# A row LSTM on one core: the gate product of the even pixels on GpSimd, the residual on VectorE, and a new written order

## The chip, the core and the metric

The kernel runs on one core of a Trainium2 chip. A core has five engines with a queue of instructions each: TensorE (PE in the profile; its weight loads stand apart as PEld), VectorE (DVE), ScalarE (ACT), GpSimd (POOL) and SyncE (SP), which here only issues the DMA transfers. The engines wait for each other through semaphores. Tiles lie in SBUF, or in PSUM, into which TensorE writes. The metric is the device time of one execution in microseconds, as the median of several runs. The profile shows another single execution, with its own time.

## What is computed

The input `x` is 8 images of 96 channels and 128 x 128 pixels in fp32. It is normalised in groups of three channels, goes through an LSTM that walks down the rows, and the LSTM's output is added to `x`:

```python
def step(carry, row_in):                       # one image row at a time
    h, c = carry
    ss = conv1d(h, W_ss, padding=1) + b_ss     # 3 taps along the row, 96 -> 384 channels
    gates = ss + row_in                        # row_in: masked 1x3 convolution of the normalised row
    f, i, o = sigmoid(...), sigmoid(...), sigmoid(...)
    g = tanh(...)
    c_new = f * c + i * g
    h_new = o * tanh(c_new)
    return ((h_new, c_new), h_new)
x = x + lstm(group_norm(x))
```

Row r needs `h` of row r-1, so the 128 rows are strictly in sequence. The mask leaves of `row_in` the left and the middle tap.

## The kernel before

**Half-steps.** The 8 images are two streams `s` of four. A half-step `n` is one row of one stream: `row, s = divmod(n, 2)`, 256 of them. While one stream's row is on TensorE, the other's is in the gates. Four rows are a block `k`, loaded from and stored to memory together.

**Tiles of the gates.** The 384 gate channels are permuted into three PSUM banks of 128 rows: A has the forget gate in rows 0 to 95, B the input gate, C the output gate, and rows 96 to 127 of each hold a third of `g`. A bank has 512 columns: even pixels of four images, then odd pixels.

**Fewer products.** The three-tap convolution for a pair of an even and an odd pixel is written with sums and differences of `h`: `vs` (even + odd), `vf` (their difference) and `vd` (two shifted differences). Product `1` (weights times `vs`) and product `2` (`vf`) go into the first and second half of a bank. Then ScalarE copies the first half to SBUF with the bias (`cp`, L508), VectorE writes the sum of both back as the even half (`lo`, L512) and the difference as the odd half (`hi`, L516), and products `0` and `3` (`vd`) are added to these halves by TensorE. The normalised row enters in the same form (`P`, `Q` before the copy, `E` after it), from operands `xs`. Channels 64 to 95 of the row share the contraction with `h` in rows 96 to 127 of `hx` ("shared" rows); channels 0 to 63 stand in `xs` ("own" images).

**Two halves of the array.** Each product is split into two of 64 contraction rows. `Lanes` deals them alternately to the upper and the lower half of TensorE's array, which work side by side. A half-step has 33 such products, each two records in the profile. Where both halves add into one bank, a wait keeps them in sequence.

**The written order.** Within the main loop nothing is planned by a scheduler: `PERIOD` (L678) lists every instruction of a half-step, and `do` (L698) issues them in that order to the engines' queues. A name is a part and a tile: `1A` is product 1 of tile A; `fg` is `forget`, f * c; `gt` is `gated`, i * g; `ce` is `cell`, c = f * c + i * g; `th` is its tanh; `ou` is `output`, o * tanh, which writes `h` into `hx`; `S` is `total` (`vs`), `F` is `difference` (`vf`), `D` is `shifted` (`vd`, on GpSimd); `re` is `residual`. A trailing `a` or `b` is the half of the even or odd pixels. A prime means the half-step before, `+` the next, `*` the one after that; `S`, `F` and `D` are made for the stream's next row.

**GpSimd's queue.** In each half-step it makes `vd` (L589), adds the residual (L607), and at `W` prepares the next block (`prepare`): of one image it normalises four rows into `xw` (`widen`, L297), forms sum (L315) and differences (L316) into `xs` (`combine`), and it normalises shared rows of one image into `hx` (`normalise_shared`); in the half-steps of a block's first row, also one row of image 3. `finish` stores a block after its fourth row's residual and loads the block after the next. `shifted` waits until VectorE is done with `S` and `F`. `FIRST` spreads the preparation of the first blocks by hand over half-steps 0 to 7.

Of the kernel before, what the change touches and what calls it, by code (L numbers as in the profile page):

```python
# [8 lines left out]
AF = mybir.ActivationFunctionType  # L9
# [12 lines left out]
def kernel(  # L22
# [32 lines left out]
    nc = tc.nc  # L55
    B, C, H, W = x.shape
    P = 128
    NH = 2
    BH = B // NH
# [239 lines left out]
    def widen(engine, xw, i, n, s, k, j, lo, step=1):  # L299


        norm(
            engine,
            strided(xw[:, i, :], 0, [(step * (W + 1), n), (J + 1, 2), (1, J)]),
            (x0[:, 0, j] if s == 1 and k == lo == 0 else xr[s][:, j, lo * W : (lo + n) * W])
            .rearrange("p (r j t) -> p r t j", r=n, t=2),
            0,
            1,
            s * BH + j,
        )  # L310

    def combine(xw, n, total, differences):

        e, o = xw[:, 0:n, 0:J], xw[:, 0:n, J + 1 :]
        nc.gpsimd.tensor_add(total, e, o)  # L315
        nc.gpsimd.tensor_sub(  # L316
            differences,
            strided(xw[:, 0, :], 0, [(W + 1, n), (J, 2), (1, J)]),
            strided(xw[:, 0, :], J + 1, [(W + 1, n), (0, 2), (1, J)]),
        )  # L320

    def own_image(s, k, j):

# [11 lines left out]
            to[:, r, 1:3, lo:hi].rearrange("p t b j -> p b t j"),  # L335
        )

    normalised = {}

    def normalise_shared(engine, s, k, j, lo, hi):  # L340

        normalised[s, k] = norm(
            engine,
            strided(
                hx[s][k % 2][C:P, lo, 0, j, :],
                0,
                [(2 * BH * JP, hi - lo), (BH * JP + 1, 2), (1, J)],
            ),
            (x0[C:P, 1, j : j + 1] if s == 1 and k == lo == 0 else xt[s, k][C:P, j, lo:hi, :])
            .rearrange("p r (j t) -> p r t j", t=2),  # L350
            C,
            0,
            s * BH + j,
        )
# [17 lines left out]
    class Lanes:  # L372
# [21 lines left out]
        def wait(self, number):  # L394

            if number > self.waited:
# [5 lines left out]
                )  # L402
                self.waited = number

    lanes = Lanes()
    whole = slice(0, P)

    class HalfStep:


        def __init__(self, n):
            self.n, (self.row, self.s) = n, divmod(n, NH)
            self.ps, self.m1, self.moving, self.done, self.gates, self.th = {}, {}, {}, set(), None, None
            self.started, self.images, self.halves, self.writer = set(), {}, {}, {}
            self.hx = hx[self.s][self.row // R % 2][:, self.row % R]
            self.xs = xs[self.s][self.row // R % 2][:, self.row % R]
            self.c = cs[self.s].rearrange("p t b j -> p (t b j)")
# [102 lines left out]
            nc.scalar.activation(self.part(g, lo, hi, t), self.part(ps, lo, hi, t), AF.Tanh)  # L520


        def sigmoid(self, a):
            if self.row == 0 and a == 0:
                return
            gate = self.ps[a][0:C]
            nc.scalar.activation(gate, gate, AF.Sigmoid)  # L527

        def forget(self):
            f = self.ps[0][0:C]  # L530
# [3 lines left out]
        def gated(self, lo=0, hi=BH, t=None):  # L534
            to = self.g if self.row > 0 else self.c
            to, i, g = (self.part(ap, lo, hi, t) for ap in (to, self.ps[1][0:C], self.g))
            nc.vector.tensor_mul(to, i, g)  # L537


        def part(self, ap, lo, hi, t=None):  # L540
# [30 lines left out]
        def total(self, engine=nc.vector, lo=0, hi=BH):  # L571
            e, o = self.pair(lo, hi)
            self.last = engine.tensor_add(self.operand("vs")[:, 0, lo:hi], e, o)  # L573
            row, s = divmod(self.n + 1, NH)
            if engine is nc.vector and row >= R and row % R < 2 and (s, row // R) in normalised:
                tc.add_manual_dep(
                    self.last.ins,
                    normalised[s, row // R].ins.name,
                    mybir.DependencyInfo(mybir.DependencyClass.Sync, mybir.DependencyReason.DATA),
                    reason="the next difference finds the next rows of x normalised",  # L580
                )

        def difference(self, engine=nc.vector, lo=0, hi=BH):
            e, o = self.pair(lo, hi)
# [2 lines left out]
        def shifted(self, lo=0, hi=BH):  # L587
            h = self.hx[:, 0, lo, :]
            diff = nc.gpsimd.tensor_sub(  # L589
                self.operand("vd", 2)[:, :, lo:hi],  # L590
                strided(h, 1, [(BH * JP - 1, 2), (JP, hi - lo), (1, J)]),
                strided(h, 0, [(BH * JP + 1, 2), (JP, hi - lo), (1, J)]),
            )
            if self.last.ins.engine != E.Pool:
                tc.add_manual_dep(
                    diff.ins,
                    self.last.ins.name,
                    mybir.DependencyInfo(
                        mybir.DependencyClass.Sync, mybir.DependencyReason.SCHED_ONLY
                    ),  # L600
                    reason="GpSimd starts when VectorE is done with both SBUF reads",
                )

        def residual(self):
            s, row = self.s, self.row
            xo = xt[s, row // R][0:C, :, row % R, :].rearrange("p b (j t) -> p t b j", t=2)
            (nc.gpsimd if 2 * row + s < last else nc.vector).tensor_add(xo, xo, self.h)  # L607

    def store(s, k, lo, hi):
        nc.sync.dma_start(  # L610
# [6 lines left out]

    SHARED = (((0, 0, R), (3, 0, 1)), ((1, 0, R),), ((2, 0, R),), ((3, 1, R),))

    def own(s, *images):  # L620
        return [(own_image, s, 1, j) for j in images]

    def shared(s, k, *images):
        return [
            (normalise_shared, nc.gpsimd, s, k, *(j if isinstance(j, tuple) else (j, 0, R)))
            for j in images
        ]

    FIRST = [
        own(0, 0),  # L630
        own(0, 1),
        own(0, 2) + shared(0, 1, 0, 1),
        own(0, 3) + [(load_rows, 0, 2)] + shared(0, 1, 2, 3),
        own(1, 0, 1),
        own(1, 2) + shared(1, 1, 0, 1),
        own(1, 3) + [(load_rows, 1, 2)] + shared(1, 1, 2, 3),
        [(own_image, 0, 2, 0), (own_image, 1, 2, 0)],
    ]

    def work(n):  # L640
        if n < len(FIRST):
            return FIRST[n]
        row, s = divmod(n, NH)
        k, r = divmod(row, R)
        parts = []
        if r == R - 1 and k + 2 < NB:
            parts.append((own_image, s, k + 2, 0))
        elif r < R - 1 and k + 1 < NB:
            parts.append((own_image, s, k + 1, r + 1))
        if k + 1 < NB:  # L650
            parts += shared(s, k + 1, *SHARED[r])
        if r == R - 2 and k + 2 < NB:
            parts.append((load_rows, s, k + 2))
        return parts

    worked = set()

    def prepare(n):
        if n not in worked:
            worked.add(n)  # L660
            for part, *args in work(n):
                part(*args)

    def finish(n):
        prepare(n)
# [18 lines left out]
    SPLIT = ("taC", "gt", "ce", "th", "ou")  # L684
    PARTS = {
# [317 lines left out]
```

## Time and profile before

| | us |
|---|---|
| median of 3 runs | 2023.72 (2023.52 to 2024.3) |
| the profiled execution, its own time | 2027.04 |
| its span | 2025.2 |
| TensorE busy | 1923.3 |
| VectorE busy | 1529.1 |
| ScalarE busy | 1494.9 |
| GpSimd busy | 1473.1 |
| granted TensorE clock | 0.997 |

A group of the profile has the line of the code, the engine, the operation, the names of the written and read tiles with buffer numbers left out, their shape, and count, busy time and mean duration. A timeline gives the start in us from the span's start, the duration, and the instructions merged if neighbours are alike (`x2`); in brackets stands the idle time before, with the instruction that ended it. Records of one engine may overlap[...]. TensorE's busy time says little alone: its records overlap in pairs.

### The profile page before, as it was taken

To read this page: it belongs to the slowest core of one execution; us is meant where nothing else is said; L and a number is where in the kernel's file an instruction comes from. 1 tells how busy PE (TensorE), PEld (TensorE's weight loads), DVE (VectorE), ACT (ScalarE), POOL (GpSimd) and SP (SyncE) were. 2 spreads that over 40 slices of the span, in tenths; PEclk is the share of its full clock that TensorE was granted. 3 is DMA by queue.
4 is the path that set the end of the run, shared out by engine and by line. 5 is a ranking of instruction groups with operands and counts; after the bars stand their busy time and mean duration, and the time that the engine had idled before them with its cause. 6 is when DMAs were issued, how large, how long until landed. Compare 5 with 4: busy or idle time off the path is not lost.

```text
span 2025.2 us, 44842 instructions
## 1 busy us (share of the span) xinstructions
PE 1923.3 (95%) x16936; PEld 1831.0 (90%) x16936; DVE 1529.1 (76%) x3996; ACT 1494.9 (74%) x3161; POOL 1473.1 (73%) x1712
## 2 busy tenths in 40 slices
PE   0289999999999999999999999999999999999998
PEld 0178999999999999999999999999999999999997
DVE  5767777777777777777777777777777777777776
ACT  3776777777777777777777777777777777777776
POOL 3348777777777777777777777777777777777752
PEclk9989999999999999999999999999999999999999
DMA  9994333444334334433433443343344333434411
GB/s 374 424 310 100 98 103 91 112 115 104 82 89 113 92 101 115 113 83 82 110 95 95 116 116 95 79 100 96 93 116 116 96 82 96 107 92 106 116 33 32
DMA packets 103382, 237.11 MB, mean 117 GB/s; under 512 B 5952, under 2 KB 8896, under 8 KB 97280
## 3 DMA queue, kind: packets, MB, share of 16 engines
q1 hardware_dynamic: 103168, 234.25, 42.0%
q8 instruction: 135, 2.21, 0.5%
q14 instruction: 79, 0.65, 0.1%
HBM read 183.90 MB, written 50.33 MB: 116 GB/s over the span
## 4 chain that ended last, share of the span: by engine, by line
PE 93%; DMA 4%; ACT 2%; DVE 1%; issue 0%; SPq 0%; POOL 0%; DVEq 0%; POOLq 0%
PE ps L442 92%; DMA piece<-in_x_dram 3%; DMA xs<-in_x_dram 1%; ACT piece L216 1%; PE ps L174 0%; ACT piece L217 0%; DVE bst L876 0%; ACT hx L295 0%; ACT piece L295 0%; DVE hx L560 0%; ACT xs L216 0%; ACT xs L217 0%; SPq L864 0%; PE pv L251 0%; DVE ps L516 0%
## 5 line engine op out<-in xcount | busy, mean ns | idle before, releaser
L442 PE MATMUL ps<-vd,wl 64*128 64x256 f32 (+1 forms) x6096 | 1390.9, 379 | 0.3
L442 PEld LDWEIGHTS ps<-vd,wl 64*128 64x128 f32 (+1 forms) x6096 | 1028.4, 186 | 45.7 <-issue 2.4
L442 PE MATMUL ps<-vs,wm 64*128 64x256 f32 (+1 forms) x3052 | 775.1, 380 | 4.9 <-POOL vs L573 4.4
L442 PE MATMUL ps<-vf,wm 64*128 64x256 f32 (+1 forms) x3052 | 766.3, 377 | 0.0
L527 ACT ACTIVATE ps<-ps 96x512 f32<-96x512 f32 x766 | 441.6, 577 | 356.2 <-PE ps L442 348.1
L442 PE MATMUL ps<-xs,wx 64*128 64x256 f32 x3080 | 637.8, 377 | 11.1 <-POOL xs L315 11.1
L589 POOL TENSOR_TENSOR vd<-hx 128x512 f32<-128x512 f32 x257 | 266.7, 1038 | 388.5 <-PE ps L442 384.8
L442 PEld LDWEIGHTS ps<-xs,wx 64*128 64x128 f32 x3080 | 494.0, 187 | 14.2 <-POOL xs L315 11.6
L520 ACT ACTIVATE g<-ps 32x256 f32<-32x256 f32 (+1 forms) x1021 | 468.6, 482 | 26.7 <-PE ps L442 6.3
L442 PEld LDWEIGHTS ps<-vf,wm 64*128 64x128 f32 (+1 forms) x3052 | 475.4, 187 | 11.0 <-PE ps L442 0.4
L442 PEld LDWEIGHTS ps<-vs,wm 64*128 64x128 f32 (+1 forms) x3052 | 459.6, 186 | 21.6 <-POOL vs L573 5.4
L512 DVE TENSOR_TENSOR ps<-m,ps 128x256 f32<-128x256 f32 x768 | 326.0, 425 | 192.5 <-ACT m L508 182.0
L442 PE MATMUL ps<-xs,wt 64*128 64x256 f32 x1530 | 453.2, 377 | 0.6 <-DVE ps L516 0.6
L508 ACT ACTIVATE m<-ps,wl 128x256 f32<-128x256 f32 x766 | 361.6, 474 | 90.9 <-PE ps L442 84.3
L532 DVE TENSOR_TENSOR ps<-ps,c 96x512 f32<-96x512 f32 x254 | 176.8, 696 | 232.9 <-PE ps L442 226.9
L607 POOL TENSOR_TENSOR x<-x,hx 96x512 f32<-96x512 f32 x255 | 330.8, 1297 | 6.7 <-DVE hx L560 6.7
L516 DVE TENSOR_TENSOR ps<-m,ps 128x256 f32<-128x256 f32 x768 | 300.8, 422 | 1.3 <-PE ps L442 1.2
L442 PEld LDWEIGHTS ps<-xs,wt 64*128 64x128 f32 x1530 | 280.0, 186 | 12.8 <-DVE ps L516 1.0
L316 POOL TENSOR_TENSOR xs<-xw 128x512 f32<-128x512 f32 (+1 forms) x254 | 270.9, 1067 | 0.0
L297 POOL TENSOR_SCALAR hx<-x,rstd,nmr 32x384 f32<-32x384 f32 (+2 forms) x312 | 225.8, 724 | 33.2 <-DMA x<-in_x_dram 1.1
L297 POOL TENSOR_SCALAR xw<-xr,rstd,nmr 128x512 f32<-128x512 f32 x252 | 205.6, 816 | 7.1 <-DVE nmr L289 6.5
L537 DVE TENSOR_TENSOR g<-ps,g 96x256 f32<-96x256 f32 x507 | 189.0, 413 | 3.8 <-ACT g L520 3.8
(91 smaller groups left out, 1223.1 us busy)
## 6 DMA issues: line engine op xcount, KB each, us to landing
xr<-in_x_dram SPq DMA_DIRECT2D x124, 512.0 KB, 6.4
x<-in_x_dram SPq DMA_DIRECT2D x63, 768.0 KB, 6.1
out_dram<-x SPq DMA_DIRECT2D x62, 768.0 KB, 4.6
xs<-in_x_dram SPq DMA_DIRECT2D x30, 1024.0 KB, 12.3
piece<-in_x_dram SPq DMA_DIRECT2D x16, 1024.0 KB, 12.3
x<-in_x_dram SPq DMA_DIRECT2D x62, 256.0 KB, 3.2
xs<-in_x_dram SPq DMA_DIRECT2D x4, 512.0 KB, 8.7
out_dram<-x SPq DMA_DIRECT2D x2, 576.0 KB, 3.7
```

Of the source, the lines that this page charges most:

```text
L297: return engine.tensor_scalar(dst, src, scale, shift, ALU.mult, ALU.add)
L316: nc.gpsimd.tensor_sub(differences, strided(xw[:, 0, :], 0, [(W + 1, n), (J, 2), (1, J)]), strided(xw[:, 0, :], J + 1, [(W + 1, n), (0, 2) ...
L442: made = nc.tensor.matmul(self.ps[a][:, bass.ts(half, HB)][:, cols], weights[rows, bass.ts(a, P)], rhs[rows, cols], start=new, stop=False, ...
L508: nc.scalar.activation(self.m1[a], m1, AF.Identity, bias=column)
L512: nc.vector.tensor_add(self.ps[a][:, 0:HB], self.m1[a], self.ps[a][:, HB:])
L516: nc.vector.tensor_sub(hi, self.m1[a], hi)
L520: nc.scalar.activation(self.part(g, lo, hi, t), self.part(ps, lo, hi, t), AF.Tanh)
L527: nc.scalar.activation(gate, gate, AF.Sigmoid)
L532: nc.vector.tensor_mul(f, f, self.c)
L537: nc.vector.tensor_mul(to, i, g)
L589: diff = nc.gpsimd.tensor_sub(self.operand("vd", 2)[:, :, lo:hi], strided(h, 1, [(BH * JP - 1, 2), (JP, hi - lo), (1, J)]), strided(h, 0, ...
L607: (nc.gpsimd if 2 * row + s < last else nc.vector).tensor_add(xo, xo, self.h)
```

## The change

- **Even pixels' gate product on GpSimd.** `sigmoid` takes pixels; B's is done in two halves, odd first (`siBb'`, `siBa'`). The even half is written to a new SBUF tile `i` (GpSimd doesn't read PSUM here), and `gated` for the even pixels runs on GpSimd and writes `g`.
- **Residual on VectorE.** `residual` runs on VectorE from half-step 2 on. In VectorE's queue it stands after `S`, `F` and `hiC`, ahead of `fg`. The first GpSimd instruction of the preparation after it is held until it has ended (`hold`, `residuals`). `total` loses its wait for normalised rows.
- **The preparation in pieces.** `W1`, `W2`, `W3` issue widen, sum and differences of an image apart; `U` issues the shared rows on GpSimd, `X` those on ScalarE, for the half-step two back. GpSimd's queue is now `vd`, widen, shared rows, sum, even gate product, differences.
- **New written order.** `PERIOD` is rewritten; the tanh of A goes to the end of the period, B's own product is taken two half-steps ahead (`QB*`), and `S` stands before `F`.
- **First blocks.** `FIRST` is spread anew; three normalisations of shared rows are on ScalarE (`beside`), and block 2's first image of stream 1 is prepared in half-steps 9, 11 and 13 (`LATER`).

```diff
-        "2A hiC' siA' D'' 1B 1A taA' 2B fg' 3C' 1A 0C' re'' taB' 2A 2B EC' 1B cpA 0C' 2C W loA cpB "
-        "3C' 1C siB' loB PB+ QA+ hiA taCb' 2C hiB taCa' 0A gtb' 1C siC' gta' EA 0B ceb' cpC 3A PA+ "
-        "cea' thb' PC+ 3B loC tha' QC+ oub' EB oua' QB+ 3A F' 3B 0A S' 0B"
+        "1A hiC' D'' X siBb' 1B 2A siBa' 2B 0C' siA' 2A re'' 3C' taB' 1A 1B fg' W1 0C' 2B cpA 3C' "
+        "2C loA cpB U W2 EC' 1C loB PB+ PA+ taCa' hiA 1C taCb' QA+ hiB gta' 2C siC' gtb' 3A 3B EA "
+        "ceb' cpC EB cea' 0A thb' W3 loC 0B tha' PC+ oub' 0A oua' 3B 3A S' 0B QB* F' taA QC+"
...
-            gate = self.ps[a][0:C]
-            nc.scalar.activation(gate, gate, AF.Sigmoid)
+            gate = self.part(self.ps[a][0:C], lo, hi, t)
+            if t == 0 and self.n > NH:
+                self.even_input = self.tile("i", (C, HB))
+                to = self.even_input.rearrange("p (b j) -> p b j", b=BH)
+            else:
+                to = gate
+            nc.scalar.activation(to, gate, AF.Sigmoid)
...
-            nc.vector.tensor_mul(to, i, g)
+            if t == 0 and self.even_input is not None:
+                i = self.even_input.rearrange("p (b j) -> p b j", b=BH)
+                nc.gpsimd.tensor_mul(to, i, g)
+            else:
+                nc.vector.tensor_mul(to, i, g)
...
-            (nc.gpsimd if 2 * row + s < last else nc.vector).tensor_add(xo, xo, self.h)
+            if self.n < NH:
+                nc.gpsimd.tensor_add(xo, xo, self.h)
+            else:
+                residuals.append(nc.vector.tensor_add(xo, xo, self.h))
...
-            row, s = divmod(self.n + 1, NH)
-            if engine is nc.vector and row >= R and row % R < 2 and (s, row // R) in normalised:
-                tc.add_manual_dep(
...
+    def hold(made, until):
+        if until.ins.engine != E.Pool:
+            tc.add_manual_dep(
...
+    spread = own(1, 1, 0, 1)
     FIRST = [
-        own(0, 0),
-        own(0, 1),
-        own(0, 2) + shared(0, 1, 0, 1),
-        own(0, 3) + [(load_rows, 0, 2)] + shared(0, 1, 2, 3),
-        own(1, 0, 1),
-        own(1, 2) + shared(1, 1, 0, 1),
-        own(1, 3) + [(load_rows, 1, 2)] + shared(1, 1, 2, 3),
-        [(own_image, 0, 2, 0), (own_image, 1, 2, 0)],
+        ([], own(0, 1, 0), []),
+        (shared(0, 1, 0), own(0, 1, 1), []),
+        (beside(0, 1, 1) + shared(0, 1, 2), own(0, 1, 2), []),
+        (beside(0, 1, 3) + shared(1, 1, 0), own(0, 1, 3), [spread[0], (load_rows, 0, 2)]),
+        (beside(1, 1, 1) + shared(1, 1, 2), own(1, 1, 1), [spread[1]]),
+        (shared(1, 1, 3), own(1, 1, 2), [spread[2]]),
+        ([], own(1, 1, 3), [(load_rows, 1, 2)]),
+        ([], own(0, 2, 0), []),
     ]
+    LATER = dict(zip((9, 11, 13), own(1, 2, 0, 1)))
...
+    def prepare(n, which="123"):
+
+        channels, image, rest = worked.setdefault(n, [list(parts) for parts in work(n)])
+        now = []
+        for name, engine in (("X", nc.scalar), ("U", nc.gpsimd)):
+            if name in which:
+                now += [part for part in channels if part[1] is engine]
+                channels[:] = [part for part in channels if part[1] is not engine]
+        for i in "123":
+            if i in which and int(i) <= len(image) and image[int(i) - 1]:
+                now.append(image[int(i) - 1])
+                image[int(i) - 1] = None
+        if image.count(None) == len(image) and n not in closed:
+            closed.add(n)
+            now += rest
+        for part, *args in now:
+            made = part(*args)
+            if made is not None and made.ins.engine == E.Pool and residuals:
+                hold(made, residuals[-1])
+                residuals.clear()
...
-            if name == "W":
-                prepare(n - 1)
+            if name in "UX":
+                if n >= NH:
+                    prepare(n - NH, name)
+                continue
+            if name[0] == "W":
+                prepare(n - 1 + name.count("+") - name.count("'"), name.strip("W+'"))
                 continue
```

More of the change, by code (lines that the diff above doesn't have):

```diff
@@ L299, in widen @@
     def widen(engine, xw, i, n, s, k, j, lo, step=1):
-        norm(
+        return norm(
             engine,
@@ L310, in widen, with add_pixels, subtract_pixels @@
         )
-    def combine(xw, n, total, differences):
-        e, o = xw[:, 0:n, 0:J], xw[:, 0:n, J + 1 :]
-        nc.gpsimd.tensor_add(total, e, o)
+    def add_pixels(xw, n, total):
+        nc.gpsimd.tensor_add(total, xw[:, 0:n, 0:J], xw[:, 0:n, J + 1 :])
+    def subtract_pixels(xw, n, differences):
         nc.gpsimd.tensor_sub(
@@ L320, in combine @@
         )
+    def combine(xw, n, total, differences):
+        add_pixels(xw, n, total)
+        subtract_pixels(xw, n, differences)
     def own_image(s, k, j):
@@ L336, in own_row @@
         )
-    normalised = {}
     def normalise_shared(engine, s, k, j, lo, hi):
-        normalised[s, k] = norm(
+        return norm(
             engine,
@@ L403, in wait @@
                 self.waited = number
+    def hold(made, until):
+        if until.ins.engine != E.Pool:
+            tc.add_manual_dep(
+                made.ins,
+                until.ins.name,
+                mybir.DependencyInfo(
+                    mybir.DependencyClass.Sync, mybir.DependencyReason.SCHED_ONLY
+                ),
+                reason="GpSimd starts when VectorE is done with both SBUF reads",
+            )
+    residuals = []
     lanes = Lanes()
@@ L414, in __init__ @@
             self.started, self.images, self.halves, self.writer = set(), {}, {}, {}
+            self.even_input = self.last = None
             self.hx = hx[self.s][self.row // R % 2][:, self.row % R]
@@ L520, in tanh, with sigmoid @@
             nc.scalar.activation(self.part(g, lo, hi, t), self.part(ps, lo, hi, t), AF.Tanh)
-        def sigmoid(self, a):
+        def sigmoid(self, a, lo=0, hi=BH, t=None):
             if self.row == 0 and a == 0:
                 return
-            gate = self.ps[a][0:C]
-            nc.scalar.activation(gate, gate, AF.Sigmoid)
+            gate = self.part(self.ps[a][0:C], lo, hi, t)
[5 more added lines that the diff above has]
+            nc.scalar.activation(to, gate, AF.Sigmoid)
         def forget(self):
@@ L573, in total @@
             self.last = engine.tensor_add(self.operand("vs")[:, 0, lo:hi], e, o)
-            row, s = divmod(self.n + 1, NH)
-            if engine is nc.vector and row >= R and row % R < 2 and (s, row // R) in normalised:
-                tc.add_manual_dep(
[L577 to L581, printed above, removed]
         def difference(self, engine=nc.vector, lo=0, hi=BH):
@@ L593, in shifted @@
             )
[L594 to L602, printed above, removed]
+            hold(diff, self.last)
         def residual(self):
@@ L618, with own, shared, beside @@
     SHARED = (((0, 0, R), (3, 0, 1)), ((1, 0, R),), ((2, 0, R),), ((3, 1, R),))
-    def own(s, *images):
-        return [(own_image, s, 1, j) for j in images]
-    def shared(s, k, *images):
+    def own(s, k, j, buffer=0):
+        to, wide = xs[s][k % 2], xw[buffer]
+        return (
+            (widen, nc.gpsimd, wide, 0, R, s, k, j, 0),
+            (add_pixels, wide, R, to[:, :, 0, j, :]),
+            (subtract_pixels, wide, R, to[:, :, 1:3, j, :]),
+        )
+    def shared(s, k, *images, engine=nc.gpsimd):
         return [
-            (normalise_shared, nc.gpsimd, s, k, *(j if isinstance(j, tuple) else (j, 0, R)))
+            (normalise_shared, engine, s, k, *(j if isinstance(j, tuple) else (j, 0, R)))
             for j in images
         ]
+    def beside(s, k, *images):
+        return shared(s, k, *images, engine=nc.scalar)
+    spread = own(1, 1, 0, 1)
     FIRST = [
-        own(0, 0),
-        own(0, 1),
-        own(0, 2) + shared(0, 1, 0, 1),
-        own(0, 3) + [(load_rows, 0, 2)] + shared(0, 1, 2, 3),
-        own(1, 0, 1),
-        own(1, 2) + shared(1, 1, 0, 1),
-        own(1, 3) + [(load_rows, 1, 2)] + shared(1, 1, 2, 3),
-        [(own_image, 0, 2, 0), (own_image, 1, 2, 0)],
+        ([], own(0, 1, 0), []),
[6 more added lines that the diff above has]
+        ([], own(0, 2, 0), []),
     ]
+    LATER = dict(zip((9, 11, 13), own(1, 2, 0, 1)))
     def work(n):
@@ L644, in work @@
         k, r = divmod(row, R)
[L645 to L662, printed above, removed]
+        ahead, image = (k + 2, 0) if r == R - 1 else (k + 1, r + 1)
+        return (
+            shared(s, k + 1, *SHARED[r]) if k + 1 < NB else [],
+            own(s, ahead, image) if ahead < NB else (),
+            ([(load_rows, s, k + 2)] if r == R - 2 and k + 2 < NB else [])
+            + ([LATER[n]] if n in LATER else []),
+        )
+    worked = {}
+    def prepare(n, which="123"):
[17 more added lines that the diff above has]
+                residuals.clear()
+    closed = set()
     def finish(n):
@@ L678 @@
     PERIOD = (
-        "2A hiC' siA' D'' 1B 1A taA' 2B fg' 3C' 1A 0C' re'' taB' 2A 2B EC' 1B cpA 0C' 2C W loA cpB "
-        "3C' 1C siB' loB PB+ QA+ hiA taCb' 2C hiB taCa' 0A gtb' 1C siC' gta' EA 0B ceb' cpC 3A PA+ "
-        "cea' thb' PC+ 3B loC tha' QC+ oub' EB oua' QB+ 3A F' 3B 0A S' 0B"
+        "1A hiC' D'' X siBb' 1B 2A siBa' 2B 0C' siA' 2A re'' 3C' taB' 1A 1B fg' W1 0C' 2B cpA 3C' "
+        "2C loA cpB U W2 EC' 1C loB PB+ PA+ taCa' hiA 1C taCb' QA+ hiB gta' 2C siC' gtb' 3A 3B EA "
+        "ceb' cpC EB cea' 0A thb' W3 loC 0B tha' PC+ oub' 0A oua' 3B 3A S' 0B QB* F' taA QC+"
     )
     PIXELS = {"a": (0, BH, 0), "b": (0, BH, 1)}
-    SPLIT = ("taC", "gt", "ce", "th", "ou")
+    SPLIT = ("taC", "siB", "gt", "ce", "th", "ou")
     PARTS = {
```

## The prediction

> **What bounds the kernel now.** I read the page first, for the engine that is never idle and the chain that ended last.
>
> ```profile
> span 2025.2 us, 44842 instructions
> PE 1923.3 (95%) x16936; PEld 1831.0 (90%) x16936; DVE 1529.1 (76%) x3996; ACT 1494.9 (74%) x3161; POOL 1473.1 (73%) x1712
> PE 93%; DMA 4%; ACT 2%; DVE 1%; issue 0%; SPq 0%; POOL 0%; DVEq 0%; POOLq 0%
> ```
>
> TensorE carries 93% of the chain; the others are a quarter idle. A busy TensorE may still hide lost time, since its records overlap, so the table of stretches gives the true rate.
>
> ```profile
> 202.35:1999.00 1796.65, 1796.65 (x16164) 1726.21 (x16166) 1378.08 (x3674) 1349.50 (x2939) 1365.95 (x1504) 1.00 0.38 97
> ```
>
> After the stretch come its length and the busy time of TensorE, with its number of records: 16,164 matmul records in 1796.65 us, without a pause. A half-step has 33 products of two records, so 16164/66 = 244.9 half-steps, 7.336 us each. The timeline of TensorE then shows what a half-step needs and what it loses.
>
> ```profile
> 1003.69 0.38 PE L442 MATMUL ps<-xs,wt 64*128 64x256 f32 x1
> 1003.73 0.38 PE L442 MATMUL ps<-vs,wm 64*128 64x256 f32 x1
> 1003.91 0.38 PE L442 MATMUL ps<-xs,wt 64*128 64x256 f32 x1
> 1003.94 0.38 PE L442 MATMUL ps<-vs,wm 64*128 64x256 f32 x1
> 1005.42 0.59 PE L442 MATMUL ps<-vf,wm 64*128 64x256 f32 x2
> 1005.77 0.45 PE L442 MATMUL ps<-vd,wl 64*128 64x256 f32 x1
> 1005.85 0.41 PE L442 MATMUL ps<-vs,wm 64*128 64x256 f32 x1
> 1006.06 0.38 PE L442 MATMUL ps<-vd,wl 64*128 64x256 f32 x1
> ```
>
> Records start two at a time (one in each half of the array's rows), every 0.216 us: 33 x 0.216 = 7.13 us. The missing 0.20 us is at 1005.77: the first `vd` product of tile A (`0A`) leaves its half of the array empty for a slot and a half. The timeline of VectorE says why.
>
> ```profile
> 1004.39 0.90 DVE L512 TENSOR_TENSOR ps<-m,ps 128x256 f32<-128x256 f32 x2 [0.70 <-ACT m L508]
> 1005.20 0.76 DVE L516 TENSOR_TENSOR ps<-m,ps 128x256 f32<-128x256 f32 x2
> 1006.53 0.74 DVE L547 TENSOR_TENSOR c<-ps,g 96x256 f32<-96x256 f32 x2
> ```
>
> The odd sum of A (`hiA`, first L516) ends at 1005.20 + 0.42 = 1005.62, and `0A` starts 0.15 later. Before it VectorE waits for ScalarE's copy `cpA`, that one for TensorE's `2A`. So TensorE waits once per half-step for its own result, come back over ScalarE and VectorE. GpSimd is not in this loop:
>
> ```profile
> 1001.90 1.04 POOL L589 TENSOR_TENSOR vd<-hx 128x512 f32<-128x512 f32 x1 [1.55 <-PE ps L442]
> 1002.90 1.30 POOL L607 TENSOR_TENSOR x<-x,hx 96x512 f32<-96x512 f32 x1
> 1004.18 0.81 POOL L297 TENSOR_SCALAR xw<-xr,rstd,nmr 128x512 f32<-128x512 f32 x1
> 1005.07 0.65 POOL L315 TENSOR_TENSOR xs<-xw 128x256 f32<-128x256 f32 x1
> ```
>
> It idles 1.55 us before each `vd` (the bracket names TensorE, but `vd` starts 0.17 after VectorE's second sum, its real releaser).
>
> [...]
>
> ```profile
> 200.66 0.42 DVE L585 TENSOR_TENSOR vf<-hx 128x256 f32<-128x256 f32 x1
> 201.00 1.29 DVE L573 TENSOR_TENSOR vs<-hx 128x256 f32<-128x256 f32 x1
> 200.70 1.31 POOL L316 TENSOR_TENSOR xs<-xw 128x512 f32<-128x512 f32 x1
> 169.69 0.44 DVE L585 TENSOR_TENSOR vf<-hx 128x256 f32<-128x256 f32 x1
> 168.69 1.95 POOL L297 TENSOR_SCALAR hx<-x,rstd,nmr 32x512 f32<-32x512 f32 x2
> ```
>
> `vf` was first, so GpSimd's L316 took 1.31 instead of 1.07 (+0.24); the next sum `vs` then lost and took 1.29 instead of 0.42, ending 0.28 after GpSimd. At 169.69 `vf` began 0.09 after the second of the two L297 (it starts at 170.64 - 1.04 = 169.60) and still won: the pair took 1.95, not 0.81 + 0.09 + 0.82 (+0.23). [...]here 256 columns take 0.64 against 0.42, 1.5 times.
>
> **The change, part by part.** I count from the start of the first of the two operand sums, now `S` (`vs`), then `F` (`vf`).
>
> *The written order.* TensorE keeps its 8468 products and the strict alternation of its row halves. What moves is the distance between a result and its use. The first products that need the odd sums are now `3A` and `3B`. From the last product that `cpA` waits for to `3A` there are 13 products, from the last `2B`, that `cpB` waits for, to `3B` 11: 11 x 0.216 = 2.37 us for the tighter one. The path that must fit in it: the last `2B` itself 0.59, to ScalarE 0.04, `cpB` 0.47, to VectorE 0.03, then `loB` 0.34 and `hiA` 0.34 to the next start (0.76 - 0.42), `hiB` 0.42 to its end, and 0.05 to TensorE (a product with this one wait; `0A` above has two and took 0.15): 2.28. It fits by 0.09, and for `hiA`, 0.34 earlier with two products more, by over half a microsecond. So the stall of 0.20 goes, and TensorE's own need of 7.13 remains; I add 0.01 for waits between the row halves, of which there are five a half-step, three products apart (0.648 against 0.59 + 0.06): 7.14.
>
> *Residual.* GpSimd loses 1.30 per half-step, VectorE gains 0.69 (the last half-step's residual runs there already). It is placed after `S` 0.34, `F` 0.34, `hiC` 0.33: start 1.01. Behind it is queued `fg`, which waits for the sigmoid of A until about 2.2 anyway; the residual ends at 1.70, so VectorE pays nothing. But `vd` on GpSimd starts at 0.93 (1001.90 - 1000.97), 0.08 before it, and both read SBUF twice. By the case at 169.69 the residual wins, and `vd` ends later by 0.23 + (0.69 - 0.42) = 0.50: at 0.93 + 1.04 + 0.50 = 2.47. TensorE has 2.8 us of slack for `vd`. SP's store and the two loads behind it wait for the residual, which ended 3.2 after `S` (1002.90 + 1.30 - 1000.97) and now ends 1.5 us earlier; SP's own order is the same, and the shared rows are normalised a half-step later than before, so no load has less time to land.
>
> *Gate product of the even pixels.* VectorE loses 0.33 of its queue; GpSimd gains 0.64 (nearest row L315, two inputs, 256 columns[...]; I take 0.64). It stands in GpSimd's queue between the sum and the differences of the own image, and `cea` waits for it, so **GpSimd enters the loop**: `vd` ends 2.47; widen -0.04 + 0.81; shared rows 0.09 + 0.81; sum 0.09 + 0.64; gate -0.04 + 0.64; 0.03 to VectorE: `cea` at 5.50. From `cea` to the next `S` stays as now: 1008.30 - 1006.86 = 1.44. That is 6.94, hidden under 7.14. In the half-steps of a block's first row (two of eight) the shared rows of image 3 add 0.09 + 0.46: 7.49. The next `S` is then late by 0.35 and TensorE, with some 0.1 in hand that the next half-step gives back, waits.
>
> *Sigmoid of B in two halves*: 256 instructions more on ScalarE, 2 x 0.38 for 0.57. (nearest row: tanh on 32x256 out of PSUM, 0.377). They lie where ScalarE idles 1.38 us after `cell_tanh`; cost nothing, 0.2 if that gap were gone. The dropped wait of `total` for GpSimd's normalisation costs and gains nothing: GpSimd is done 1.5 us before.
>
> *`hold`.* GpSimd's widen waits for the residual's end (1.70 + 0.17), which `vd` outlasts: nothing.
>
> *First blocks.* Three normalisations go to ScalarE, one image's three parts to half-steps 9 to 13. Half-steps 3 to 9 now take 4.5 us more than seven steady ones; I take a gain of 1, between -3 and +4, since the image's parts still meet the new gate product.
>
> *Sum.* Mean (6 x 7.14 + 2 x 7.49)/8 = 7.23, 0.108 below 7.336. Over 237 half-steps 25.6; the last 8, without next rows, 0.196 each: 1.6; start 1. Together 28. The profiled execution took 2027.04 (2025.2 its span), 3.3 above the median 2023.72. So 1999 for it, and **1996** as median.
>
> **Rivals.**
>
> *The residual loses the port (slower).* `vd` has 0.08 of a start. If that suffices, `vd` ends at 1.97, the residual at 1.97 + 0.28 + 0.27 = 2.52, widen is held to 2.69, 0.26 later than above: 7.20 and 7.75, and any semaphore step of 0.05 on GpSimd makes it 7.25 and 7.80, mean 7.39: +12, less the 3 of start and end: **2033**. For it: start order decides the lock at 201.00. Against: 169.69, same lead, VectorE won. The change is slower from a GpSimd chain 0.26 longer than mine: 6 x 7.20 + 2 x 7.75 = 8 x 7.336.
>
> *GpSimd is not delayed at all.* If it had read most of its data, or its 0.64 is 0.5, all half-steps are 7.14: 0.196 x 245 + 1 = 49 less, **1975**. For it: 0.20 of clean idle on TensorE to win. Against: both collisions cost GpSimd 0.23.
>
> *The stall only moves.* With 33 products, the row halves swap roles each half-step; if the swap, not `hiA`, costs the 0.20, it stays: **2023**. Against: `0A` starts right upon `hiA`'s end everywhere.
>
> **How the numbers follow.** Forecast 0.48 (1984 to 2011, the gate at 0.54 to 0.75), second rival 0.17, third 0.10, slower rival 0.25. A measurement here can tell 0.2%, 4 us. Faster 0.65, same 0.10, slower 0.25. The range from 1972 to 2034 leaves out about 2 in 10, half of the slower rival and the edge of the second.
>
> **What would show it.** TensorE's records at 0.216 without a gap before `3A` and `3B`; `vd` at about 1.5 us; the residual on VectorE at 0.69 (it won) or 1.5 (it lost); `cea` waiting for GpSimd in a quarter of the half-steps alone, and TensorE's `vs` products for `S` there. Wrong if `cea` waits in all, or if `vd` stays at 1.04 with the residual at 0.69.

## The result: 0.75% slower, and the profile after

| | before | after |
|---|---|---|
| median, us | 2023.66 (2023.52 to 2024.3) | 2038.38 (2037.78 to 2041.36) |
| profiled execution, us | 2027.04 | 2038.46 |
| its span, us | 2025.2 | 2036.7 |
| GpSimd busy, us | 1473.1 | 1329.7 |
| VectorE busy, us | 1529.1 | 1812.6 |
| mean half-step, half-steps 10 to 247, us | 7.336 | 7.404 |

The ratio after to before is 1.0075 (95% interval 1.0058 to 1.0092): a small loss, but clear of noise. The forecast was 1996, a gain, so it was wrong in sign; the rival "the residual loses the port" gave 2033. "The port" is a name for an effect that the traces show: where a VectorE sum of two SBUF tiles and a GpSimd instruction overlap, as at 201.00 in the kernel before, one of them can take longer (`vs` there 1.29 instead of 0.42). What causes it isn't seen in them.

The page of the changed kernel, the lines that answer to the first fence of the prediction:

```profile
span 2036.7 us, 45537 instructions
PE 1935.3 (95%) x16936; PEld 1847.4 (91%) x16936; DVE 1812.6 (89%) x3997; ACT 1555.9 (76%) x3417; POOL 1329.7 (65%) x1708
PE 82%; DVE 7%; POOL 5%; DMA 4%; issue 1%; ACT 1%; SPq 0%; POOLq 0%; DVEq 0%; ACTq 0%
L621 DVE TENSOR_TENSOR x<-x,hx 96x512 f32<-96x512 f32 x254 | 371.1, 1461 | 0.0
L297 POOL TENSOR_SCALAR xw<-xr,rstd,nmr 128x512 f32<-128x512 f32 x252 | 205.8, 817 | 181.9 <-DVE x L621 174.9
L574 DVE TENSOR_TENSOR c<-ps,g 96x256 f32<-96x256 f32 x508 | 207.1, 419 | 55.3 <-POOL g L562 36.0
```

TensorE's share of the chain fell from 93% to 82%, and VectorE and GpSimd came in. The residual (L621) has a mean of 1461 ns, not 690 as in the kernel before (its last one, at 2021.12). GpSimd's widen (L297) idles 0.7 us for the residual before 243 of its 252 runs. VectorE's cell sum (L574) waits for GpSimd's gate product. The table of waits counts the longer ones:

```profile
POOL xw L297 <- DVE x L621: 174.9, 243, 0.7
DVE c L574 <- POOL g L562: 36.0, 63, 0.7
PEld ps L460 <- DVE vs L600: 24.2, 63, 0.8
```

The waits of VectorE for the gate product and of TensorE for `S` are 63 each there, about a quarter of the 256 half-steps. The table leaves the shortest waits out, and the timeline shows that the gate product is late more often. In a half-step without the extra row (the first line is of GpSimd, the second of VectorE):

```profile
1009.90 0.72 POOL L562 TENSOR_TENSOR g<-i,g 96x256 f32<-96x256 f32 x1
1010.13 0.95 DVE L574 TENSOR_TENSOR c<-ps,g 96x256 f32<-96x256 f32 x2
```

The two cell sums take 0.95, not the 0.75 of a pair without a pause: the second one, `cea`, starts at 1010.66, right upon the gate product's end at 1010.62. The same holds in six of eight half-steps. In two of the six `cea` is 0.6 to 0.76 later than VectorE could have begun it, in the other four 0.16 to 0.19.

From TensorE's timeline, the distance from the first `vs` product of a half-step to that of the next goes 7.28, 7.23, **7.61, 7.87**, 7.33, 7.27, 7.30, 7.30 and repeats so, within 0.04, every eight, mean 7.40. The two long ones are those of a block's first row, where GpSimd normalises a row of image 3 as well. One of them, on VectorE (start, duration, instruction, and in the bracket the wait before it):

```profile
1033.72 0.42 DVE L600 TENSOR_TENSOR vs<-hx 128x256 f32<-128x256 f32 x1
1034.06 0.42 DVE L604 TENSOR_TENSOR vf<-hx 128x256 f32<-128x256 f32 x1
1034.40 0.42 DVE L534 TENSOR_TENSOR ps<-m,ps 128x256 f32<-128x256 f32 x1
1034.73 1.48 DVE L621 TENSOR_TENSOR x<-x,hx 96x512 f32<-96x512 f32 x1
...
1040.11 0.42 DVE L574 TENSOR_TENSOR c<-ps,g 96x256 f32<-96x256 f32 x1 [0.52 <-POOL g L562]
...
1041.56 0.43 DVE L600 TENSOR_TENSOR vs<-hx 128x256 f32<-128x256 f32 x1
```

and the same on GpSimd:

```profile
1034.62 1.04 POOL L608 TENSOR_TENSOR vd<-hx 128x512 f32<-128x512 f32 x1 [1.50 <-DVE vf L604]
1036.39 0.81 POOL L297 TENSOR_SCALAR xw<-xr,rstd,nmr 128x512 f32<-128x512 f32 x1 [0.72 <-DVE x L621]
1037.30 1.37 POOL L297 TENSOR_SCALAR hx<-x,rstd,nmr 32x512 f32<-32x512 f32 x2
1038.75 0.64 POOL L314 TENSOR_TENSOR xs<-xw 128x256 f32<-128x256 f32 x1
1039.35 0.72 POOL L562 TENSOR_TENSOR g<-i,g 96x256 f32<-96x256 f32 x1
```

`vd` starts 0.11 before the residual and takes its plain 1.04; the residual takes 1.48 and ends 0.55 after it (1036.21); the hold lets the widen start at 1036.39. The gate product ends at 1040.07, `cea` starts at 1040.11, and the next `S` 1.45 later: 7.84 after the one before.

**Where the time went**, in the two profiled executions. The eleventh half-step starts 4.8 earlier (its first `vs` product at 205.00, not 209.77). The 238 half-steps from there are 0.068 longer each: +16.2. The last seven, for which GpSimd has nothing to prepare, gain 1.3 together, and the end after the last one's start takes 1.3 longer. The sum, +11.4, is the spans' difference of 11.5 but for roundings; that of the medians is 14.7, since the profiled execution of before was 3.3 above its median and that of after is at its own.

### The profile page after: what moved, and what is told of

Read it like the earlier page. It is cut to its first block, busy times and chain, and to the rows that moved or that the text cites. A ratio compares the mean times of both kernels' runs of the same rounds, so it can differ in the third digit from the quotient of the medians.

```text
span 2036.7 us, 45537 instructions
## 1 busy us (share of the span) xinstructions
PE 1935.3 (95%) x16936; PEld 1847.4 (91%) x16936; DVE 1812.6 (89%) x3997; ACT 1555.9 (76%) x3417; POOL 1329.7 (65%) x1708
## 4 chain that ended last, share of the span: by engine, by line
PE 82%; DVE 7%; POOL 5%; DMA 4%; issue 1%; ACT 1%; SPq 0%; POOLq 0%; DVEq 0%; ACTq 0%
PE ps L460 82%; DMA xs<-in_x_dram 4%; DVE x L621 2%; POOL hx L297 2%; POOL xw L297 1%; DVE bst L919 1%; POOL xs L314 1%; DVE hx L587 1%; POOL g L562 1%; DVE vs L600 1%; DVE c L574 1%; DVE ps L530 1%; DVE ps L534 1%; DVE vf L604 1%; PE ps L174 0%
## 5 line engine op out<-in xcount | busy, mean ns | idle before, releaser
L460 PE MATMUL ps<-vd,wl 64*128 64x256 f32 (+1 forms) x6096 | 1275.6, 381 | 0.8 <-DVE ps L534 0.2
L460 PEld LDWEIGHTS ps<-vd,wl 64*128 64x128 f32 (+1 forms) x6096 | 943.4, 186 | 29.9 <-issue 1.7
L460 PE MATMUL ps<-vs,wm 64*128 64x256 f32 (+1 forms) x3052 | 703.3, 384 | 5.9 <-POOL vs L600 4.0
L460 PE MATMUL ps<-xs,wx 64*128 64x256 f32 x3080 | 676.8, 377 | 11.1 <-POOL xs L314 11.1
L530 DVE TENSOR_TENSOR ps<-m,ps 128x256 f32<-128x256 f32 x768 | 325.8, 425 | 98.7 <-ACT m L526 81.7
L550 ACT ACTIVATE ps<-ps 96x512 f32<-96x512 f32 x767 | 388.7, 507 | 14.4
L460 PE MATMUL ps<-xs,wt 64*128 64x256 f32 x1530 | 384.6, 377 | 0.0
L621 DVE TENSOR_TENSOR x<-x,hx 96x512 f32<-96x512 f32 x254 | 371.1, 1461 | 0.0
L297 POOL TENSOR_SCALAR xw<-xr,rstd,nmr 128x512 f32<-128x512 f32 x252 | 205.8, 817 | 181.9 <-DVE x L621 174.9
L574 DVE TENSOR_TENSOR c<-ps,g 96x256 f32<-96x256 f32 x508 | 207.1, 419 | 55.3 <-POOL g L562 36.0
L297 POOL TENSOR_SCALAR hx<-x,rstd,nmr 32x512 f32<-32x512 f32 (+2 forms) x309 | 222.8, 721 | 32.6 <-DVE x L621 2.2
L579 ACT ACTIVATE th<-c 96x256 f32<-96x256 f32 (+1 forms) x510 | 203.7, 412 | 49.7 <-DVE c L574 37.9
```

What stands on the lines that cost most here:

```text
L297: return engine.tensor_scalar(dst, src, scale, shift, ALU.mult, ALU.add)
L460: made = nc.tensor.matmul(self.ps[a][:, bass.ts(half, HB)][:, cols], weights[rows, bass.ts(a, P)], rhs[rows, cols], start=new, stop=False, ...
L530: nc.vector.tensor_add(self.ps[a][:, 0:HB], self.m1[a], self.ps[a][:, HB:])
L550: nc.scalar.activation(to, gate, AF.Sigmoid)
L574: nc.vector.tensor_add(c, f, g)
L579: nc.scalar.activation(self.part(self.th, lo, hi, t), self.part(self.c, lo, hi, t), AF.Tanh)
```

## The experiments

Each number is a median; ratios are to the kernel before on the same chip (2024.2 to 2024.5 there).

**1. Without the residual.** It is left out from half-step 2 on, and with it the hold, so the output lacks it.

```diff
-            else:
-                residuals.append(nc.vector.tensor_add(xo, xo, self.h))
```

> Left out from the second step of each batch half on: the residual sum (and with it the hold on it), so this part of the computation is missing. Theory A (the residual starts 0.10 us after vd, waits for the port to vd's end, and the hold passes its end on to GpSimd, whose gate product TensorE then waits for in two of eight half-steps): GpSimd's 0.72 us wait before the widen goes, every half-step falls to TensorE's own 7.23 of this written order (the last eight half-steps of the changed kernel), that is 237 x (7.40 - 7.23) = 40 less: 1998 us. Theory B (VectorE, 89% busy with a residual of 1.46 us, is itself too late with its own later work): the same 1998, since that goes too. Theory C (the new written order itself costs the time, and the residual is hidden): 2036 to 2040.

Measured 1993.85 us (ratio 0.9848, 0.9831 to 0.9864). All steady half-steps are 7.229, those of a block's first row too. The new written order can run at 7.229, and the residual on VectorE, with the hold that hangs on it, costs the changed kernel 44.5 us. Theory C falls; A and B can't be told apart by this run.

**2. The even gate product back on VectorE; 3. the residual back on GpSimd; 4. both.**

```diff
-            if t == 0 and self.n > NH:             # 2 and 4
+            if False:
...
-            if self.n < NH:                        # 3 and 4
-                nc.gpsimd.tensor_add(xo, xo, self.h)
-            else:
-                residuals.append(nc.vector.tensor_add(xo, xo, self.h))
+            (nc.gpsimd if 2 * row + s < last else nc.vector).tensor_add(xo, xo, self.h)
```

> The even pixels' gate product goes back to VectorE (in PSUM as before), the residual stays on VectorE after the odd sum of C. Theory A: the residual still takes about 1.46 us and GpSimd's widen still waits for it, but nothing on TensorE's way waits for GpSimd any more; all half-steps alike at 7.23 to 7.26: 1997 to 2005 us. Theory B: VectorE has 0.33 us more per half-step and is what is late: 7.45 to 7.75 in all half-steps, 2050 to 2115 us. Theory C: 2036 to 2040.

> The residual goes back to GpSimd (1.30 us, after vd), the even gate product stays on GpSimd. Theory A: GpSimd's own chain from vd to the gate product is 1.30 - 0.72 = 0.58 us longer than in the changed kernel, and it sets the period in all half-steps: about 7.8 in six of eight, 8.3 in two, mean 7.93: 2150 to 2170 us. Theory B: VectorE is relieved of 1.46 us: about 1998. Theory C: 2036 to 2040.

> Residual back on GpSimd and even gate product back on VectorE: what is left of the change is the written order, the sigmoid of B in two halves and the spread of the first blocks. Theory A: TensorE's own 7.23 in all half-steps, 1995 to 2003 us, faster than both kernels. Theory C: the written order itself costs the time, 2024 or more. If the even gate product on VectorE makes cea late in this order: 7.3 to 7.45, 2015 to 2045.

| | us | ratio (95%) | half-steps |
|---|---|---|---|
| gate product back | 2057.83 | 1.0164 (1.0149 to 1.0179) | 7.44 to 7.51 |
| residual back | 2156.16 | 1.0652 (1.0636 to 1.0668) | 7.6 to 7.8, two of eight 8.35 |
| both back | 2057.67 | 1.0164 (1.0149 to 1.0179) | 7.44 to 7.51 |

*Residual back* is theory A's 2150 to 2170: with 1.30 on GpSimd in front of the gate product every half-step is GpSimd's (VectorE waits for that product 241 times there, 63 times in the changed kernel). Theory B, which had 1998 there, falls for the changed kernel. The other two missed theory A's 2000. *Gate product back* lies in theory B's range of 2050 to 2115, and *both back* in theory C's "2024 or more", which run 1 had ruled out. With the gate product on VectorE something else is late, and alike with and without the residual there (2057.83 and 2057.67), so it isn't the port. VectorE's timeline with both back shows it:

```profile
1002.22 0.97 DVE L530 TENSOR_TENSOR ps<-m,ps 128x256 f32<-128x256 f32 x2 [0.61 <-ACT m L526]
1003.10 0.75 DVE L534 TENSOR_TENSOR ps<-m,ps 128x256 f32<-128x256 f32 x2
1003.76 0.74 DVE L564 TENSOR_TENSOR g<-ps,g 96x256 f32<-96x256 f32 x2
...
1006.32 0.42 DVE L600 TENSOR_TENSOR vs<-hx 128x256 f32<-128x256 f32 x1
...
1009.65 0.97 DVE L530 TENSOR_TENSOR ps<-m,ps 128x256 f32<-128x256 f32 x2 [0.61 <-ACT m L526]
```

In the new order VectorE is in a loop with TensorE: from the first even sum (L530) to `S` 4.10 us without a pause, from `S` over TensorE's products and ScalarE's copy to the next even sum 3.33: 7.43. The gate product of the even pixels is 0.33 of the first stretch; without it the loop would be about 7.1 (an estimate, 7.43 - 0.33), under TensorE's 7.229. So theory B's mechanism, a late VectorE, is real with that product on VectorE, and in these runs the new order pays only with the product on another engine.

**5. Without the hold.** Only the order between the engines is dropped.

```diff
-                hold(made, residuals[-1])
                 residuals.clear()
```

> Only the hold of GpSimd's widen on the residual's end is dropped (it orders engines, no data). Theory A1 (the residual has waited for the port since 0.1 us after vd's start and gets it when vd ends; the widen is then held up only until the residual has read, some 0.3 us, not 0.72): the heavy half-steps lose most of their 0.4 to 0.6, mean 7.27: about 2007 us. Theory A2 (the widen, next in GpSimd's queue, takes the port again at once and the residual waits for it too, to about 3.3 us after the first sum): GpSimd is on time, but the forget product, and behind it the even sums, come 0.5 us late in every half-step: mean 7.6 to 7.9, 2085 to 2155 us.

Measured 2012.24 us (0.9940, 0.9925 to 0.9954), A1's mechanism, a little more than its 2007. The heavy half-steps are 7.31 and 7.54, the one behind them 7.33, the other five 7.23. GpSimd's timeline:

```profile
1007.20 1.04 POOL L608 TENSOR_TENSOR vd<-hx 128x512 f32<-128x512 f32 x1 [1.52 <-DVE vf L604]
1008.22 1.31 POOL L297 TENSOR_SCALAR xw<-xr,rstd,nmr 128x512 f32<-128x512 f32 x1
```

The residual (1007.37 to 1008.79 here) ends 0.55 after `vd`, as with the hold. It is the widen, which starts right upon `vd`'s end, that takes longer: 1.31 instead of 0.81. It ends 2.33 after `vd` starts, with the hold 2.58. So the hold is the smaller part of the 0.72: without it the widen still loses 0.50, and the hold adds some 0.25 to its end. Over the run that is 26 us.

**6. The gate product first.** In the written order the own image's sum moves from ahead of the even gate product to behind it.

```diff
-        "2C loA cpB U W2 EC' 1C loB PB+ PA+ taCa' ...
-        "ceb' cpC EB cea' 0A thb' W3 loC 0B ...
+        "2C loA cpB U EC' 1C loB PB+ PA+ taCa' ...
+        "ceb' cpC EB cea' 0A thb' W2 W3 loC 0B ...
```

> One edit of the written order: on GpSimd the even gate product goes ahead of the own image's sum, which follows it and comes directly before the differences. The collision and the hold stay. Theory A (what costs is only that the gate product ends late on GpSimd): it starts 0.55 to 0.65 earlier in the heavy half-steps, and 0.2 earlier in the others, where the tanh it needs becomes the limit; light half-steps 7.23, heavy ones 7.23 to 7.35: 1997 to 2005 us, with the residual still at 1.46 and the 0.72 wait still before the widen. If the late residual itself or the forget product behind it costs the time: 2030 to 2040, as the changed kernel.

Measured **1998.97 us** (0.9876, 0.9861 to 0.9891): 1.2% faster than before and 39 us faster than the changed kernel. The collision and the hold are still there, and no longer matter, as the table of waits shows:

```profile
POOL xw L297 <- DVE x L621: 175.3, 243, 0.7
...
POOL g L562 <- ACT g L538: 94.2, 192, 5.2
```

The widen waits as long as ever. But now the gate product is early: in three quarters of the half-steps it waits itself, 0.5 on average, for ScalarE's tanh, and VectorE no longer waits for it. All steady half-steps are 7.23. What cost the time was that one product's place in a late queue, 0.60 behind the sum, which nothing waits for soon. Together with *residual back*, where a longer queue ahead of the product cost as much as theory A said, this shows theory A.

**7. gate_first without the hold**, edits 5 and 6 together.

> gate_first without the hold on the widen. Theory A: GpSimd is on time in gate_first already, so its 0.72 us wait costs nothing there: the same within 0.2%, 1995 to 2003 us. If the hold still cost in gate_first: 1985 or less. If the hold were needed to keep the widen from taking the port from the residual: 2020 or more.

Measured 1999.23 us (0.9876, 0.9861 to 0.9891): the hold costs nothing there.

**8. Image 3's extra row on ScalarE.**

```diff
-    SHARED = (((0, 0, R), (3, 0, 1)), ((1, 0, R),), ((2, 0, R),), ((3, 1, R),))
+    SHARED = (((0, 0, R),), ((1, 0, R),), ((2, 0, R),), ((3, 1, R),))
...
-            shared(s, k + 1, *SHARED[r]) if k + 1 < NB else [],
+            shared(s, k + 1, *SHARED[r]) + (beside(s, k + 1, (3, 0, 1)) if r == 0 else [])
+            if k + 1 < NB else [],
```

> The first row of image 3 (32x2x64), which only two of eight half-steps normalise on GpSimd, goes to ScalarE, which is idle 0.9 us before the tanh of A. Theory A: the 0.38 and 0.64 of the heavy half-steps go; all are like the light ones now, 7.27 to 7.30, or less since nothing is left to give back: 2005 to 2014 us. If the loss isn't GpSimd's lateness: 2036 to 2042.

Measured 2025.41 us (1.0005, 0.9996 to 1.0014), short of the 2005 to 2014 expected: the two half-steps are now 7.63 each. ScalarE's timeline in one of them:

```profile
1028.95 0.59 ACT L538 ACTIVATE g<-ps 32x512 f32<-32x512 f32 x1 [1.11 <-PE ps L460]
1029.57 0.50 ACT L295 ACTIVATE hx<-x,nmr,rstd 32x128 f32<-32x128 f32 x1
1030.09 0.36 ACT L550 ACTIVATE ps<-ps 96x256 f32<-96x256 f32 x1
```

ScalarE is idle *ahead of* the tanh of A. The row stands behind it, in the run of tanh, sigmoids and copies without a pause that ends in `cpB` and the even sums. It put 0.5 into that run: the first even sum starts 4.08 after `S` here, and 3.56 in the half-step before. TensorE got 0.40 of it. The 1.11 of idle time in front of the tanh's wait were no room for the row written behind it.

**9. vd delayed by a small memset; 10. vd after hiC.** Both ask which of the two instructions takes longer.

```diff
+            if self.n > 2 * NH:                            # 9
+                hold(nc.gpsimd.memset(tiny, 0.0), self.last)
...
-            nc.vector.tensor_sub(hi, self.m1[a], hi)       # 10
+            made = nc.vector.tensor_sub(hi, self.m1[a], hi)
+            if a == order["C"]:
+                odd_of_c.append(made)
...
-            hold(diff, self.last)
+            hold(diff, odd_of_c[-1] if odd_of_c and self.n > 2 * NH else self.last)
```

> A tiny memset (32x1) on GpSimd between its wait for the second operand sum and vd, so that vd starts after the residual, not before it. If the start order decides the port: the residual takes 0.69 again and vd is stretched by about 0.5, to about 2.6 us after the first sum; the widen follows at once, about 0.1 earlier than in the changed kernel: mean about 7.36, 2025 to 2032 us. If GpSimd wins the port whatever the order: the residual stays at 1.4 to 1.5, all of it some 0.1 later: 2040 to 2055.

Measured 2031.08 us (1.0034, 1.0020 to 1.0047), inside the first range for another reason: the memset took 0.09 but didn't delay `vd`, which started 0.53 after `vf` with it and 0.57 without. The residual still started 0.13 after `vd` and took 1.45. The start order wasn't changed, so nothing was told of the port. The 0.04 by which `vd` came earlier was passed on (the mean half-step is 7.37, not 7.40), and that is the 7 us by which this run is faster than the changed kernel.

> The changed kernel with one dependency more: vd on GpSimd waits for the odd sum of C (hiC), not for vf, and so starts about 0.24 us after the residual on VectorE instead of 0.10 before it. If the start order decides who has the port: the residual takes 0.69 (ends 1.70 after the first sum) and vd, blocked until then, ends at 2.5 to 2.75, where the widen follows without a wait; in the changed kernel the widen starts at 2.69. Mean 7.30 to 7.42, 2015 to 2043 us; the sign of the whole isn't told by this, the residual's 0.69 is. If GpSimd takes the port whatever the order, as residual_first left open: residual at 1.6 or more, widen 0.2 to 0.3 later than in the changed kernel, mean 7.5 to 7.65, 2060 to 2095.

Measured 2024.77 us (1.0004, 0.9995 to 1.0012). VectorE's residual and GpSimd's `vd` and widen:

```profile
1006.02 0.68 DVE L624 TENSOR_TENSOR x<-x,hx 96x512 f32<-96x512 f32 x1
```

```profile
1006.26 1.35 POOL L611 TENSOR_TENSOR vd<-hx 128x512 f32<-128x512 f32 x1 [1.72 <-DVE ps L535]
1007.59 0.81 POOL L297 TENSOR_SCALAR xw<-xr,rstd,nmr 128x512 f32<-128x512 f32 x1
```

With 0.24 of a lead the residual is at 0.68 again, `vd` is stretched by 0.31, and the widen starts 2.58 after `S`. Of these two instructions the one that starts first keeps its plain time, here and in the changed kernel, where `vd` takes 1.04 and the residual 1.42 to 1.51. But the kernel is only as fast as before, not faster: five of eight half-steps are 7.23, those of a block's first row 7.51 and 7.72, the one behind them 7.33.

**11. and 12. What is TensorE's 7.229 made of?** The sum 33 x 0.216 gives 7.13. Both runs stand on gate_first (`W2` is moved as there); in run 12 `ZA+` is a product with weights of zero.

```diff
-        ... PC+ oub' 0A oua' 3B 3A S' 0B QB* F' taA QC+"
+        ... PC+ oub' QB* QC+ oua' 0A 3B S' 3A 0B F' taA"          # fillers_moved
+        ... PC+ oub' QB* ZA+ oua' 0A 3B S' 3A 0B F' taA QC+"      # one_more_product
```

> gate_first with QB and QC, which no result of this half-step feeds, ahead of the second 0A and 3B, so that these two stand five products, not three, behind the product of the other row half they wait for. Theory W (the 0.10 us that TensorE's half-step is above 33 x 0.216 is lost to those two waits, which point in opposite directions on consecutive products): 7.13 to 7.17, 1973 to 1985 us. Theory X (it is lost because with 33 products the row halves change roles every half-step, and the three other waits at a distance of three change direction with them): 7.23 as before, 1995 to 2002.

> fillers_moved with a 34th product in each half-step (weights of zero, so nothing is added to the sums), and QC back at the end. A product more costs 0.216 of TensorE's time on the two row halves. Theory X: with an even number the row halves keep their roles, all waits at a distance of three point the same way, and the 0.10 goes: 17 x 0.432 = 7.344, 0.115 more than 7.229: 2024 to 2030 us. Theory W: 0.216 more than fillers_moved's half-step, if that is 7.13, the same 7.344; if fillers_moved is 7.23: 7.445, 2048 to 2054.

Measured 2064.94 us (1.0202, 1.0185 to 1.0219) and 2064.01 (1.0197, 1.0181 to 1.0212). Both missed all expectations, and for one reason: with the fillers ahead of them the last products of A end later against the start of the next half-step (by two products in run 11, by one in run 12), and the tanh of A, which waits for them, is late. ScalarE idles 1.45 before it in both (1.11 in gate_first), and half-steps with 33 and with 34 products are alike at 7.49, so TensorE's rate wasn't what bound. The two theories can't be told apart by them. The trace of gate_first shows where the 0.10 is: with the two halves of the array taken in turn, the products of each start 0.216 apart but for one, at 0.32, in the last run of `vd` products before the next half-step (1010.24 and 1010.56 there; 1004.24 and 1004.55 in the changed kernel). Why that one is late stays open.

## Why the prediction was wrong

**The step that failed first** is in *Residual*: "By the case at 169.69 the residual wins." It lost, in every steady half-step, with `vd` ahead by 0.08 to 0.17: 1.42 to 1.51 for the residual, 1.04 for `vd`. The case at 169.69 had the same lead, but another GpSimd instruction, a TENSOR_SCALAR; `vd` is a TENSOR_TENSOR. The trace of before has no case of a TENSOR_TENSOR on GpSimd with so short a lead over one of the operand sums. The changed kernel has one in its start-up, `xs` against the sum `vs`, on GpSimd and on VectorE:

```profile
157.90 0.64 POOL L314 TENSOR_TENSOR xs<-xw 128x256 f32<-128x256 f32 x1
```

```profile
157.92 0.91 DVE L600 TENSOR_TENSOR vs<-hx 128x256 f32<-128x256 f32 x1
```

A lead of 0.02 was enough there: `vs` took 0.91 instead of 0.42, `xs` its plain 0.64. In the result and in vd_later, too, the TENSOR_TENSOR that started first kept its plain time (`vd` 1.04, the residual 0.68). I set a single case over the one at 201.00, where `vs` started 0.30 behind a TENSOR_TENSOR and lost, without asking how the two differed.

**Its consequence**, `hold` at nothing, fell with it: the residual now ended after `vd`, and the widen waited 0.72, some 0.25 of it for the hold (run 5). From there the forecast's path to `cea` can be followed in the light half-steps (1004.80 the start of `S`): the widen starts at 2.67, not 2.43, and the gate product takes 0.72, not 0.64; with small gaps `cea` comes at 5.86, not 5.50, and 5.86 + 1.44 = 7.30 is what they measure. The rival had worked out this mechanism: 7.25 and 7.80, mean 7.39. That it also came so near in size is in part luck, since its allowance of 0.05 made up for the gate product, which it had at 0.64.

**The port alone is not all of it.** vd_later is the forecast's own case as nearly as a run shows it: the residual wins, and still the kernel is no faster than before (1.0004). Winning the port (0.68 for the residual there) is worth some 14 of the 42 us between the forecast 1996 and 2038. The rest lies mostly in three terms that were too small. `vd`, when it loses, ends 0.90 after the residual there, which makes 2.60 of the forecast's 2.47; the gate product took 0.72, not 0.64; and TensorE's own need was 7.229, not 7.14.

**The written order**: the stall at `0A` went, and the first products on the odd sums start without a gap. With nothing late the half-step is 7.229 (runs 1, 6 and 7, and the last half-steps of the changed kernel). Where nothing else binds, the 0.09 above 7.14 takes up to 0.09 x 245 = 22 us of the gain, and so gate_first, where GpSimd delays nothing, is at 1999 and not at the 1975 of the rival "GpSimd is not delayed at all". I had put 0.01 on the waits between the row halves; whether these cost the 0.10 is open.

**Gate product**: GpSimd did enter the loop. The prediction named a wait of `cea` in a quarter of the half-steps as the sign of its own case, and the table of waits seems to show that; but by the timeline `cea` waits in six of eight, near its "wrong if `cea` waits in all". The residual at "1.5 (it lost)" told the cases apart. That VectorE is 0.33 shorter was booked as queue time; runs 2 and 4 show that the new order needs it.

**First blocks**: 1 us was forecast for half-steps 3 to 9, and they gained 2.0 (53.9 instead of 55.9), inside the range of -3 to 4. The other 2.8 of the 4.8 lie ahead of half-step 3, which starts at 151.08 in the changed kernel and between 150.64 and 153.10 in its variants, against 153.88 in the one execution of before that was profiled; how much of that is the change can't be told. Which of the edits brings the 2.0 wasn't tried. **Sigmoid in halves** wasn't tried alone. No cost of it shows where GpSimd is on time, but the cover named for it was the wrong one: run 8 put 0.50 more into the same run of ScalarE and lost 0.40, so that run has about 0.10 to spare (an estimate, the difference of the two), not the idle time ahead of it.

## What to carry to other kernels

When a result that the critical path waits for is moved to an engine on which it takes longer (0.72 on GpSimd, 0.41 on VectorE), put it first in that engine's queue that its inputs allow, ahead of work that is needed later: here that alone was worth 39 us of 2038. Before you trust that an engine is waited for in a few places only, look at the timeline: waits of under 0.2 us that the table left out set the time of half of the half-steps here. Where a VectorE sum of two SBUF tiles can start just behind a GpSimd instruction, as the residual did here (1.46 instead of 0.69), ask which instruction that is, and cost the losing case first if the precedent is of another kind of instruction. A hold that "costs nothing" has to be costed for the case in which the instruction it waits for is late.

## What the runs showed of the hardware that was not expected

- The lead, by the starts in the trace, with which GpSimd's instruction kept its plain time differed with its kind. TENSOR_TENSOR did with 0.02 (`vs` 0.91 instead of 0.42, at 157.92 in the changed kernel) and with 0.08 to 0.17 (residual 1.42 to 1.51 instead of 0.69, 243 times). TENSOR_SCALAR did not with 0.09 in before (at 169.69: `vf` 0.44; GpSimd 1.04 instead of 0.81). It did with 0.26 there (at 1734.70: `vf` 0.47 instead of 0.42, GpSimd 0.46). Each of the cases outside the 243 is one event.
- A VectorE instruction that had started behind one GpSimd instruction went ahead of GpSimd's next one, though that followed at once: in run 5 the widen behind `vd` took 1.31 and 1.24 instead of 0.81 in the two half-steps at 1008.22 and 1015.46, and in the changed kernel the differences behind the sum at 157.90 took 1.25 instead of 1.07 (at 158.50).
- Between the residual and `vd` the price of losing came out alike in both directions: the loser ended after the winner by its own plain time less about 0.14. The residual (0.69 plain) ends 0.54 to 0.56 after `vd` in the changed kernel, and in vd_later `vd` (1.04 plain) ends 0.91 and 0.89 after the residual (at 1006.26 and 1013.42). That the residual grew by 0.8 and `vd` by only 0.31 and 0.37 comes from what was left of the winner: 0.87 to 0.97 of `vd`, 0.44 and 0.52 of the residual.
